# Transposes moved from TensorE to VectorE blocks and SBUF copies, with channels-first block ends in layer 0

## The chip, the cores and the metric

The kernel runs on one core of a Trainium2 chip. A core has four compute engines: TensorE (PE) for products, VectorE (DVE), ScalarE (ACT) and GpSimd (POOL). A fifth one, SyncE (SP), issues all copies of this kernel from one queue; 16 DMA engines carry them out. Everything is float32. The metric is device time in microseconds (us).

## The reference, cut to what matters

`x` is 4 images of 128 channels by 4096 positions. Layer 0 is an attention over all positions with a gate. Layer 1 is a second attention whose queries and keys are the same tensor, then a recurrence over all positions.

```python
# layer 0 (per image; n, m run over 4096 positions)
xn   = group_norm(x, 32 groups)
v, g = split(sigmoid(bn(Wvg @ xn)))             # 128 channels each
q, k = bn(Wq @ xn) * 64**-0.5, bn(Wk @ xn)      # 64 channels each
attn = softmax(einsum('bdn,bdm->bnm', q, k))
x    = x + bn(Wp @ (einsum('bcm,bnm->bcn', v, attn) * g))
# layer 1, on tokens t = transpose(x): (image, position, channel)
h  = layernorm(t);  q = h @ W
t  = t + softmax(q @ q.T) @ h
Wx = batch_norm(layernorm(t) @ Wf.T)            # over all images and positions
# y_i = sigmoid(Wx_i + y_(i-1) @ V.T), i over positions in order
x  = transpose(t + ys)
```

## The kernel before, in words

The work on each image is cut into 8 blocks of 512 query positions (`QB`; four tiles of 128, `NQ`). The images follow each other: `group_norm`, `project` (q, k, v, gate), `layer0`, `layer1`. After the last image comes the recurrence, called the scan here.

**Layer 0** (`attention`). For each block n there are 16 pair steps. In each, PE makes two score products `ps` (L186), ACT takes the exponential `e` (L189), VectorE adds it into `acc` (L198) for the denominators, and PE weighs the values into `o` (L326), two steps behind (`LAG`). Five buffers hold `e`. The end of a block is cut into closures that `finish` puts into the queue `pending`: `sums`, `residual`, `tokens`, `turn`, `queries`. The loop takes one out in every second pair step, in the middle of the next block, so that their work lies among the products. Every engine runs its own instructions in order; a waiting one holds up all behind it on that engine. The order on each engine is laid out when the program is built.

In `sums`, the 512 denominators are brought onto partitions by four products with one column of ones (`md`, L214). `residual` turns the four 128x128 tiles of x + bias on PE (`mx`, L351). `tokens` projects with positions first, four products (`mt`, L357), scales by the reciprocal denominators, stores the tokens into HBM (`t_d`) and normalises them (`h`). `turn` turns `h` back on PE (`mh`, L372), and `queries` makes the layer-1 queries `qt` from it (`mq`, L377). After the last block the queue is flushed with nothing beside it.

**Layer 1.** Scores are symmetric, so only the tiles a <= n of the 8x8 grid of blocks are computed (`ps`, L502; `e`, L508; `o`, L404). An off-diagonal tile is also used transposed: VectorE turns `e` in 32x32 blocks into `dd` (L513), 16 copies within SBUF put the blocks in place as `tt` (L532), and PE multiplies by it (`ot`, L417), while VectorE sums its rows into `slots` (L422). There are 28 such tiles per image. A finished block queues `tokens` (4 turns on PE, `mt`, L456), `result` (4 turns, `mr`, L467, and a copy to `t2_d` in HBM), `turn` (4 turns, `mh`, L475) and `inputs` (`mw`, L480, into `wxs`). These steps are taken from the same queue, also during the next image's `project`.

**The scan.** Positions are cut into 128 stretches of 32 that run side by side for all images; each starts from a state got by 12 warm-up steps on the end of the stretch before it. In each of the 44 steps and for each half of the images, PE adds `vt @ y` to a PSUM bank that VectorE has filled with the scaled inputs (L598), and ACT takes the sigmoid (L615).

Of the kernel before, what the change touches and what calls it, by code (L numbers as in the profile page):

```python
# [9 lines left out]
F32 = mybir.dt.float32  # L10
I32 = mybir.dt.int32
AF = mybir.ActivationFunctionType
ALU = mybir.AluOpType
# [21 lines left out]
L, W = 32, 12  # L35
# [13 lines left out]
def conv_attn_hybrid_kernel(  # L49
# [14 lines left out]
    t_d = dram.tile([B, NB, P, NQ, C], F32, name="t_d")  # L64
# [33 lines left out]
    ones = const.tile([P, 1], F32, name="ones")  # L98
# [9 lines left out]
    def inv_sqrt(dst, var, eps):  # L108
# [6 lines left out]
        tc, x, out, t_d, t2_d,  # L115
# [6 lines left out]
    with ExitStack() as st:  # L122
        ps = st.enter_context(tc.tile_pool(name="ps_f", bufs=1, space=PSUM))
        bad = const.tile([1, 1], I32, name="bad")
        n_ok = ps.tile([1, 1], F32, tag="f", name="n_ok")
        nc.tensor.matmul(n_ok, lhsT=par_ok[:, 0:1], rhs=ones, start=True, stop=True)
        nc.vector.tensor_scalar(bad, n_ok, P - 0.5, None, ALU.is_lt)
# [9 lines left out]
def fast(  # L137
    tc, x, out, t_d, t2_d, wt, col, par, bpc, bc, ident, gavg, ones, shift, inv_sqrt, par_ok
# [5 lines left out]
    wxs = keep.tile([P, L // 2, B, G, 2], F32, name="wxs")  # L144
    bn_st = keep.tile([P, B * NB, 6], F32, name="bn_st")
    den_all = keep.tile([P, 2 * B * NT], F32, name="den_all")

    with ExitStack() as st:
# [60 lines left out]
        def denominators(acc, at, rinv):  # L209

            nc.vector.tensor_tensor(acc[:, 0, :], acc[:, 0, :], acc[:, 1, :], ALU.add)
            m = ps_m.tile([P, NQ], F32, tag="m", name="md")
            for j in range(NQ):
                nc.tensor.matmul(  # L214
                    m[:, j : j + 1], lhsT=acc[:, 0, bass.ts(j, P)], rhs=ones,
                    start=True, stop=True,
                )
            den = den_all[:, at : at + NQ]
            nc.vector.tensor_copy(den, m)
            nc.vector.reciprocal(rinv, den)  # L220

        def layernorm(src, dst):
# [3 lines left out]
            for j in range(NQ):  # L226
                s6 = stat.tile([P, 6], F32, tag="s6", name="s6")
                nc.vector.bn_stats(s6, src[:, j, :])  # L228
                nc.vector.bn_aggr(mv[:, j, :], s6)  # L229
            inv_sqrt(rstd, mv[:, :, 1], EPS_LN)  # L230
            for j in range(NQ):
                nc.vector.tensor_scalar(  # L232
                    dst[:, j, :], src[:, j, :], mv[:, j, 0:1], rstd[:, j : j + 1],
                    ALU.subtract, ALU.mult,
                )
# [75 lines left out]
        def layer0(b, gate, q, k, v):  # L311
# [20 lines left out]
            def finish(n, o, acc):  # L332
# [5 lines left out]
                rinv = stat.tile([P, NQ], F32, tag="rinv", name="rinv")  # L338
                xb = work.tile([P, QB], F32, tag="xb", name="xb", bufs=2)
                t = work.tile([P, NQ, C], F32, tag="t", name="t", bufs=2)  # L340
                ht = work.tile([P, QB], F32, tag="th", name="ht")
                nc.sync.dma_start(xb, x[b, :, cs])
                nc.gpsimd.tensor_scalar(xb, xb, bpc, None, ALU.add)  # L343

                def sums():
                    denominators(acc, b * NT + n * NQ, rinv)

                def residual():
                    m = ps_m.tile([P, NQ, P], F32, tag="m", name="mx")
                    for j in range(NQ):  # L350
                        nc.tensor.transpose(m[:, j, :], xb[:, bass.ts(j, P)], ident)  # L351
                    nc.scalar.copy(t, m)

                def tokens():
                    m = ps_m.tile([P, NQ, P], F32, tag="m", name="mt")
                    for j in range(NQ):
                        nc.tensor.matmul(  # L357
                            m[:, j, :], lhsT=og[:, bass.ts(j, P)], rhs=wt["ps"],
                            start=True, stop=True,
                        )  # L360
                    for j in range(NQ):
                        nc.vector.scalar_tensor_tensor(
                            t[:, j, :], m[:, j, :], rinv[:, j : j + 1], t[:, j, :],
                            ALU.mult, ALU.add,
                        )
                    nc.sync.dma_start(t_d[b, n], t)
                    layernorm(t, h[:, ts, :])

                def turn():
                    m = ps_m.tile([P, QB], F32, tag="m", name="mh")  # L370
                    for j in range(NQ):
                        nc.tensor.transpose(m[:, bass.ts(j, P)], h[:, n * NQ + j, :], ident)  # L372
                    nc.scalar.copy(ht, m)

                def queries():
                    m = ps_m.tile([P, QB], F32, tag="m", name="mq")
                    nc.tensor.matmul(m, lhsT=wt["a"], rhs=ht, start=True, stop=True)  # L377
                    nc.scalar.copy(qt[:, cs], m)  # L378

                pending.extend([sums, residual, tokens, turn, queries])  # L380
# [4 lines left out]
        def layer1(b, h, qt):  # L385
# [55 lines left out]
            def finish(n):  # L441
                cs = bass.ts(n, QB)
                rinv = stat.tile([P, NQ], F32, tag="rinv", name="rinv")
                t = work.tile([P, NQ, C], F32, tag="t", name="t1", bufs=2)
                h2 = work.tile([P, NQ, C], F32, tag="h2", name="h2")
                th = work.tile([P, QB], F32, tag="th", name="th")
                nc.sync.dma_start(t, t_d[b, n])

                def tokens():
                    at = (B + b) * NT + n * NQ  # L450
# [3 lines left out]
                    m = ps_m.tile([P, NQ, P], F32, tag="m", name="mt")  # L454
                    for j in range(NQ):
                        nc.tensor.transpose(m[:, j, :], oacc[:, n, bass.ts(j, P)], ident)  # L456
                    for j in range(NQ):
                        nc.vector.scalar_tensor_tensor(  # L458
                            t[:, j, :], m[:, j, :], rinv[:, j : j + 1], t[:, j, :],
                            ALU.mult, ALU.add,  # L460
                        )
                    layernorm(t, h2)

                def result():
                    m = ps_m.tile([P, QB], F32, tag="m", name="mr")
                    for j in range(NQ):
                        nc.tensor.transpose(m[:, bass.ts(j, P)], t[:, j, :], ident)  # L467
                    t2 = work.tile([P, QB], F32, tag="xb", name="t2", bufs=2)
                    nc.scalar.copy(t2, m)
                    nc.sync.dma_start(t2_d[b, :, cs], t2)  # L470

                def turn():
                    m = ps_m.tile([P, QB], F32, tag="m", name="mh")
                    for j in range(NQ):
                        nc.tensor.transpose(m[:, bass.ts(j, P)], h2[:, j, :], ident)  # L475
                    nc.scalar.copy(th, m)

                def inputs():
                    m = ps_m.tile([P, QB], F32, tag="m", name="mw")
                    nc.tensor.matmul(m, lhsT=wt["f"], rhs=th, start=True, stop=True)  # L480
                    nc.vector.bn_stats(bn_st[:, b * NB + n, :], m)
                    nc.vector.tensor_copy(
                        wxs[:, :, b, bass.ts(n, GB), :],
                        m.rearrange("p (g i s) -> p i g s", i=L // 2, s=2),
                    )

                pending.extend([tokens, result, turn, inputs])
# [62 lines left out]
        ok = stat.tile([P, 2, 2 * B * NT], F32, tag="ok", name="ok", bufs=1)  # L550
        nc.vector.tensor_scalar(ok[:, 0, :], den_all, DEN_LO, None, ALU.is_ge)
        nc.vector.tensor_scalar(ok[:, 1, :], den_all, DEN_HI, None, ALU.is_le)
        nc.vector.tensor_reduce(par_ok[:, 1:2], ok.rearrange("p a b -> p (a b)"), AX.X, ALU.min)


    with ExitStack() as st:
        scan = st.enter_context(tc.tile_pool(name="scan", bufs=1))
        ps_r = st.enter_context(tc.tile_pool(name="ps_r", bufs=1, space=PSUM))
# [3 lines left out]
        y = scan.tile([P, L // 2, B, G, 2], F32, name="y")  # L562
        state = scan.tile([P, B, G + 1], F32, name="state")
        nc.gpsimd.memset(state[:, :, 0:1], 0.0)

        HB = B // 2
        banks = [[ps_r.tile([P, 512], F32, tag=f"r{s}{i}", name="ps_r") for i in range(3)] for s in range(2)]
        for s in range(2):  # L570
            for i in range(3):
                nc.tensor.matmul(
                    banks[s][i][:, : HB * G], lhsT=ident, rhs=wxs[:, 0, :HB, :, 0],
                    start=True, stop=True, skip_group_check=True,
                )
# [8 lines left out]
        nc.vector.tensor_sub(bias, col(BETA), bias)  # L584

        halves = [slice(s * HB, (s + 1) * HB) for s in range(2)]
        steps = list(range(L - W, L)) + list(range(L))

        def bank(k, s):
            return banks[s][k % 3][:, : HB * G].rearrange("p (b g) -> p b g", g=G)  # L590

        def at(tile_, i, bs):
            return tile_[:, i // 2, bs, :, i % 2]

        def preload(k):
            if k < len(steps):
                for s, bs in enumerate(halves):
                    nc.vector.tensor_scalar(bank(k, s), at(wxs, steps[k], bs), gain, None, ALU.mult)  # L598

        todo: deque = deque()  # L600
        preload(1)
        preload(2)
        for k, i in enumerate(steps):
            for s, bs in enumerate(halves):

                dst = state[:, bs, 1:] if k == W - 1 else at(y, i, bs)
                if k == 0:
                    nc.scalar.activation(dst, at(wxs, i, bs), AF.Sigmoid, bias=bias, scale=gain)
                    continue
                before = state[:, bs, :G] if k == W else at(y, i - 1, bs)  # L610
                nc.tensor.matmul(
                    bank(k, s), lhsT=wt["vt"], rhs=before, start=False, stop=True,
# [428 lines left out]
```

## Time and profile before

| what | us |
|---|---|
| median of 3 runs (3354.44 to 3355.76) | 3355.1 |
| the profiled execution | 3355.76 |
| its span, first to last instruction | 3353.9 |
| first layer-0 score, image 0 | 54.7 |
| first layer-1 score, image 0 | 438.8 |
| first layer-0 score, image 1 | 867.0 |
| first activation of the scan | 3268.6 |

How to read it: the page's first part gives the busy time of each engine as a share of the span. The chain is the work that ended last, followed back through what released each step. In the groups, "line engine op, out<-in, shapes, xcount" is followed by busy time, mean ns of one, and idle time just before them with what ended it; busy time counts overlap once, so it can be less than count times mean. SPq in a timeline is the SP engine's queue, and its time is the time to issue copies, not to move the data. "128*128 128x512" is a product with 128 rows of contraction and a 128x512 result. A float32 product appears as two records.

### The profile page before, as it was taken

The numbers are of one execution on the slowest core, as the hardware profiler recorded it, in microseconds if no ns is written. First come the engines' busy times: TensorE is split into PE (matmuls) and PEld (weight loads), VectorE is DVE, ScalarE is ACT, GpSimd is POOL, SyncE is SP. The second block draws the span as 40 slices with busy tenths as digits, with TensorE's granted clock in tenths as the row PEclk, the third lists the DMA queues.
The fourth block names the chain that finished last, engine by engine and source line by source line (L and its number), as shares of the span: only waits on it lengthen the run. The fifth ranks groups of instructions, "written<-read, shape, count | busy, mean of one in ns | idle before, by whom it ended". The sixth has DMA issues, their size and how long they took to land.

```text
span 3353.9 us, 32409 instructions
## 1 busy us (share of the span) xinstructions
PE 3148.9 (94%) x11210; PEld 1437.9 (43%) x11210; DVE 1708.3 (51%) x2793; ACT 1171.5 (35%) x2050; POOL 144.1 (4%) x183
## 2 busy tenths in 40 slices
PE   6999999997899999999699999999979999999976
PEld 3444444443444444444344444444434444444433
DVE  4545544555555544555645554455555555345556
ACT  3443432332434333233244343323233444332324
POOL 0000000000000000000000000000000000000000
PEclk9999999998999999999899999999989999999998
DMA  1000023332000003333200001333300000233334
GB/s 41 13 10 10 10 70 90 92 91 88 10 10 13 13 13 88 91 90 92 67 7 13 13 7 35 90 95 93 102 26 13 7 13 10 63 91 92 91 97 175
DMA packets 109084, 179.24 MB, mean 53 GB/s; under 512 B 31472, under 2 KB 31984, under 8 KB 107888
## 3 DMA queue, kind: packets, MB, share of 16 engines
q1 hardware_dynamic: 108912, 177.08, 19.4%
q8 instruction: 92, 1.51, 0.2%
q14 instruction: 80, 0.66, 0.1%
HBM read 34.35 MB, written 25.17 MB: 18 GB/s over the span
## 4 chain that ended last, share of the span: by engine, by line
PE 88%; DVE 6%; ACT 2%; POOL 1%; issue 1%; DMA 1%; SPq 0%; DVEq 0%; POOLq 0%; ACTq 0%
PE o L326 26%; PE ps L186 14%; PE ps L502 14%; PE o L404 14%; PE ot L417 11%; PE mq L377 1%; PE pvg L293 1%; PE mt L357 1%; POOL rstd L111 1%; PE md L214 1%; PE mw L480 1%; PE pvg L297 1%; DMA xg<-in_x_dram 1%; DVE t L458 1%; DVE s L228 1%
## 5 line engine op out<-in xcount | busy, mean ns | idle before, releaser
L326 PE MATMUL o<-e,v 64*128 64x512 f32 x4096 | 960.1, 590 | 0.0
L198 DVE TENSOR_TENSOR acc<-acc,e 128x1024 f32<-128x1024 f32 x448 | 548.7, 1225 | 525.3 <-ACT e L189 519.5
L189 ACT ACTIVATE e<-ps 128x1024 f32<-128x1024 f32 x512 | 521.0, 1024 | 684.5 <-PE ps L186 684.5
L508 ACT ACTIVATE e<-ps,shift 128x512 f32<-128x512 f32 x576 | 391.2, 683 | 940.1 <-PE ps L502 768.3
L326 PEld LDWEIGHTS o<-e,v 64*128 64x128 f32 x4096 | 397.3, 188 | 486.6 <-issue 479.0
L502 PE MATMUL ps<-qt 128*128 128x512 f32 x1152 | 547.3, 604 | 2.7 <-ACT qt L378 2.7
L186 PE MATMUL ps<-q,k 64*128 64x512 f32 x2048 | 539.5, 608 | 9.0 <-ACT e L189 4.8
L404 PE MATMUL o<-e,h 128*128 128x512 f32 x1152 | 527.7, 592 | 0.0
L417 PE MATMUL ot<-tt,h 128*128 128x512 f32 x896 | 402.8, 592 | 0.0
L513 DVE STREAM_TRANSPOSE dd<-e 128x512 f32<-128x512 f32 x448 | 285.7, 683 | 125.1 <-ACT e L508 82.4
L502 PEld LDWEIGHTS ps<-qt 128*128 128x128 f32 x1152 | 217.6, 194 | 269.9 <-issue 240.0
L404 PEld LDWEIGHTS o<-e,h 128*128 128x128 f32 x1152 | 217.1, 191 | 260.2 <-issue 260.2
L186 PEld LDWEIGHTS ps<-q,k 64*128 64x128 f32 x2048 | 185.6, 187 | 223.1 <-issue 123.2
L417 PEld LDWEIGHTS ot<-tt,h 128*128 128x128 f32 x896 | 170.2, 190 | 214.3 <-issue 212.4
L422 DVE TENSOR_REDUCE slots<-tt 128x4 f32<-128x2048 f32 x112 | 252.9, 2258 | 2.3 <-DMA tt<-dd 1.7
L429 DVE TENSOR_TENSOR oacc<-oacc,ot 128x512 f32<-128x512 f32 x84 | 57.4, 684 | 309.7 <-PE ot L417 309.7
L232 DVE TENSOR_SCALAR h<-t,mv,rstd 128x128 f32<-128x128 f32 x256 | 73.0, 346 | 94.5 <-POOL rstd L111 94.4
L508 ACT ACTIVATION_READ_ACCUMULATOR e<-ps,shift 128x1 f32 x576 | 113.0, 196 | 0.0
L343 POOL TENSOR_SCALAR xb<-xb,bpc 128x512 f32<-128x512 f32 x32 | 57.0, 1781 | 1112.4 <-DMA xb<-in_x_dram 1112.4
L110 POOL TENSOR_SCALAR rstd<-mv 128x4 f32<-128x4 f32 x64 | 14.6, 229 | 1949.0 <-DVE mv L229 1949.0
L427 DVE COPY oacc<-ot 128x512 f32<-128x512 f32 x28 | 19.4, 692 | 139.5 <-PE ot L417 139.5
L293 PE MATMUL pvg<-w_vs,xg 128*128 128x128 f32 x256 | 42.7, 318 | 31.9 <-ACT xg L304 23.8
(112 smaller groups left out, 1510.9 us busy)
## 6 DMA issues: line engine op xcount, KB each, us to landing
tt<-dd SPq DMA_DIRECT2D x1792, 64.0 KB, 2.0
t_d<-t SPq DMA_DIRECT2D x64, 256.0 KB, 2.0
xg<-in_x_dram SPq DMA_DIRECT2D x16, 512.0 KB, 5.6
xb<-in_x_dram SPq DMA_DIRECT2D x32, 256.0 KB, 2.7
t<-t_d SPq DMA_DIRECT2D x32, 256.0 KB, 2.7
t2s<-t_d SPq DMA_DIRECT2D x4, 2048.0 KB, 14.8
out_dram<-t2s SPq DMA_DIRECT2D x4, 2048.0 KB, 15.6
w<-in_wts_dram SPq DMA_DIRECT2D x1, 512.0 KB, 3.5
```

Source lines behind the costliest of these rows:

```text
L186: nc.tensor.matmul(ps[:, h, :], lhsT=lhsT, rhs=rhs, start=True, stop=True)
L189: nc.scalar.activation(e, ps, AF.Exp, scale=scale)
L198: nc.vector.tensor_tensor(acc, acc, e, ALU.add)
L232: nc.vector.tensor_scalar(dst[:, j, :], src[:, j, :], mv[:, j, 0:1], rstd[:, j : j + 1], ALU.subtract, ALU.mult,)
L293: nc.tensor.matmul(pv[:, 0, bass.ts(i, P)], lhsT=xg[:, bass.ts(4 * ch + i, P)], rhs=wt["vs"], start=True, stop=True,)
L326: nc.tensor.matmul(o[r], lhsT=v[rs, p + h * PAIRS, :], rhs=e[rs, h, :], start=(p == 0 and h == 0), stop=(p == PAIRS - 1 and h == 1),)
L404: nc.tensor.matmul(o, lhsT=h[:, NQ * a + 2 * i + half, :], rhs=e[:, half, :], start=(a == n and i == 0 and half == 0), stop=(a == 0 and i ...
L417: nc.tensor.matmul(ot, lhsT=h[:, NQ * n + j, :], rhs=t[:, :, j, :, :].rearrange("q p k j -> q k p j"), start=(j == 0), stop=(j == NQ - 1),)
L422: nc.vector.tensor_reduce(slots[:, bass.ts(n, NQ), a], t.rearrange("q p b k j -> q b p (k j)"), AX.XY, ALU.add,)
L502: nc.tensor.matmul(ps[:, half, :], lhsT=qt[:, bass.ts(at, P)], rhs=qt[:, bass.ts(n, QB)], start=True, stop=True,)
L508: nc.scalar.activation(e[:, half, :], ps[:, half, :], AF.Exp, bias=shift, accum_out=slots[:, at, n : n + 1],)
L513: nc.vector.transpose(d.rearrange("q f b k j -> q k b f j")[:, 2 * i + half], e[:, half, :].rearrange("q (b f j) -> q b f j", b=NQ, f=NQ),)
```

## The change

All transposes of tokens leave PE. A new function `move` turns a 128x512 tile on VectorE in 32x32 blocks into `d` (two buffers), and, where a destination is given, sends 16 copies of 32 partitions x 128 elements to put the blocks in place:

```diff
+        def move(blocks, dst):
+            d = work.tile([P, 4, NQ, 32], F32, tag="d", name="d", bufs=2)
+            nc.vector.transpose(d.rearrange("q a j i -> q j a i"), blocks)
+            if dst is not None:
+                for p in range(4):
+                    for a in range(4):
+                        nc.sync.dma_start(dst[bass.ts(a, 32), p], d[bass.ts(p, 32), a])
+            return d
```

Layer 0's block end stays channels first up to the residual. One product with a full matrix of ones puts the sums on all partitions, the reciprocal is taken over 128x512, and one product projects. Two moves follow, for `t` and for `ht`:

```diff
                 def sums():
-                    denominators(acc, b * NT + n * NQ, rinv)
-                def residual():
-                    (4 transposes of xb on PE, copy by ACT into t)
+                    nc.vector.tensor_tensor(acc[:, 0, :], acc[:, 0, :], acc[:, 1, :], ALU.add)
+                    m = ps_m.tile([P, QB], F32, tag="m", name="md")
+                    nc.tensor.matmul(m, lhsT=ones, rhs=acc[:, 0, :], start=True, stop=True)
+                    rinv = work.tile([P, QB], F32, tag="h2", name="rinv")
+                    nc.vector.reciprocal(rinv, m)
+                    nc.sync.dma_start(rinv_d[b * NB + n : b * NB + n + 1, :], rinv[0:1, :])
+                    nc.vector.tensor_tensor(og, og, rinv, ALU.mult)
+                def project_out():
+                    m = ps_m.tile([P, QB], F32, tag="m", name="mt")
+                    nc.tensor.matmul(m, lhsT=wt["ps"], rhs=og, start=True, stop=True)
+                    nc.vector.scalar_tensor_tensor(xb, m, bpc, xb, ALU.add, ALU.add)
+                    move(xb.rearrange("c (j f k) -> c j f k", j=NQ, f=4), t)
                 def tokens():
-                    (4 products mt on PE, 4 scalings on VectorE)
                     nc.sync.dma_start(t_d[b, n], t)
-                    layernorm(t, h[:, ts, :])
-                def turn():
-                    (4 transposes of h on PE, copy by ACT into ht)
+                    layernorm([t[:, :, j, :] for j in range(NQ)], [...])
+                    move(h[:, ts, :].rearrange("q j (p i) -> q j p i", p=4), ht)
-                pending.extend([sums, residual, tokens, turn, queries])
+                pending.extend([sums, project_out, tokens, queries])
```

Lines in brackets stand for the removed code. The addition of the bias to `xb` on POOL goes too, and `xb` has one buffer in place of two. In layer 1 a block end has three turns by VectorE: `oacc` into `ot` (name `otk`; 16 copies), `t` straight to HBM (16 copies with runs of 128 bytes), and `h2` into `th` (16 copies):

```diff
+                def weighted():
...
+                    move(oacc[:, n, :].rearrange("c (j f k) -> c j f k", j=NQ, f=4), ot)
                 def tokens():
...
+                    d = move(t.rearrange("q p j i -> q j p i"), None)
+                    to = t2_d[b, :, cs].rearrange("(p i) (j f k) -> i p j f k", p=4, f=4, j=NQ)
+                    for f in range(4):
+                        for p in range(4):
+                            nc.sync.dma_start(to[:, p, :, f, :], d[bass.ts(f, 32), p])
+                    layernorm([t[:, :, j, :] for j in range(NQ)], [...])
+                    move(h2.rearrange("q j (p i) -> q j p i", p=4), th)
-                pending.extend([tokens, result, turn, inputs])
+                pending.extend([weighted, tokens, inputs])
```

The denominators of layer 0 are checked from the rows stored in HBM (`rinv_d`), read back before the scan. The scan has 16 warm-up steps (`W`) in place of 12, a plain layout of `wxs` and `y`, and PE in place of VectorE adds the scaled inputs:

```diff
-L, W = 32, 12
+L, W = 32, 16
-                    nc.vector.tensor_scalar(bank(k, s), at(wxs, steps[k], bs), gain, None, ALU.mult)
+        nc.vector.tensor_scalar(dgain, ident, gain, None, ALU.mult)
+                ps = ps_r.tile([P, HB, G], F32, tag=f"r{s}", name="ps_r")
+                nc.tensor.matmul(ps, lhsT=dgain, rhs=wxs[:, i, bs, :], start=True, stop=first, ...)
+                if not first:
+                    nc.tensor.matmul(ps, lhsT=wt["vt"], rhs=befores(bs), start=False, stop=True, ...)
+                nc.scalar.activation(outs(bs), ps, AF.Sigmoid, bias=bias)
```

The additions of `y` to the tokens come four together at every fourth step, in place of one a step.

## The prediction

> **What bounds the kernel now.** I read the page first: busy shares, then the chain that ended last, then the costliest groups, then the DMA issues.
>
> ```profile
> PE 3148.9 (94%) x11210; PEld 1437.9 (43%) x11210; DVE 1708.3 (51%) x2793; ACT 1171.5 (35%) x2050; POOL 144.1 (4%) x183
> PE 88%; DVE 6%; ACT 2%; POOL 1%; issue 1%; DMA 1%; SPq 0%; DVEq 0%; POOLq 0%; ACTq 0%
> ```
>
> TensorE (PE) is the bound: 94% busy and 88% of the chain. Taking products off it pays only while nothing makes it wait. The groups of instructions, shapes kept apart, price what leaves it and what comes:
>
> ```profile
> L404 PE MATMUL o<-e,h 128*128 128x512 f32 x1152 | 527.7, 592 | 0.0
> L357 PE MATMUL mt<-w_ps,og 128*128 128x128 f32 x256 | 36.9, 287 | 3.5 <-DVE og L337 3.5
> L214 PE MATMUL md<-ones,acc 128*128 128x1 f32 x256 | 33.7, 253 | 0.0
> L351 PE MATMUL mx<-ident,xb 128*128 128x128 f32 x128 | 20.9, 285 | 1.4 <-DVE den_all L219 1.4
> L513 DVE STREAM_TRANSPOSE dd<-e 128x512 f32<-128x512 f32 x448 | 285.7, 683 | 125.1 <-ACT e L508 82.4
> ```
>
> A float32 product is two records, so a 512-wide product costs 527.7/576 = 0.92 us. A 32x32-block transpose of a 128x512 tile costs VectorE 0.68 us.
>
> The resource the change leans on is not in the busy shares at all: SP's queue, which issues every copy. The timeline of SP alone, in layer 1, and the tile view of `tt`:
>
> ```profile
> 600.07 10.01 SPq L532 DMA_DIRECT2D tt<-dd  x16
> ...
> L532 SPq DMA_DIRECT2D tt<-dd x1792: 507/589/1771, 452.7 to 3231.1; - x200
> ...
> DMA to landing us min/median/max: 1.9/2.0/4.0
> ```
>
> Sixteen SBUF-to-SBUF copies keep SP for 10.0 us (0.625 us each with the gap); each lands 2.0 us after its issue. One off-diagonal tile of layer 1 gives PE 12 products (11.0 us by 0.92; 10.3 at the 0.86 of a gapless stream), so SP is already nearly full there. Its issues are 28 x 10.0 = 280 us of each image's layer 1, which lasts 428 us from its first score (438.8) to the next image's first layer-0 score (867.0).
>
> The timeline of PE at a layer-0 block end shows the room for a moved step:
>
> ```profile
> 158.24 1.16 PE L357 MATMUL mt<-w_ps,og 128*128 128x128 f32 x8
> ...
> 170.61 1.13 PE L377 MATMUL mq<-ht,w 128*128 128x512 f32 x2
> ```
>
> From `mt` to `mq` PE has 11 us of other work, in which LayerNorm and one turn are hidden.
>
> **What the Trainium skill says.** (1) "VectorE: DVE Perf Modes", The three transpose paths: VectorE turns only 32x32 blocks, so the grid of blocks needs another step, here 16 copies. The trace agrees: `dd` is followed by exactly that. (2) "DMA: Bandwidth & Descriptors", Issuing engines are not separate DMA queues: issue time on the sequencer is "usually small relative to the DMA itself". The trace differs for these copies, 10.0 us of issue against 2.0 us to land; the measurement decides. (3) "VectorE: DVE Perf Modes", Walkthrough: reciprocal is an iterative divide with repeat count 8. No wide reciprocal is in the trace. (4) "TensorE: Matmul & The Clock Gate", Part 1: after about 3.4 us idle the array runs at half rate until it has been busy about as long. The trace agrees: after the layer boundary 12 score records took 8.21 us instead of 12 x 0.43 = 5.2.
>
> **The change part by part.** Sums are against the profiled execution (3355.8 us, span 3353.9), 0.7 us above the median.
>
> *Layer 0, PE work.* Gone per block: md, mx, mt and mh, (33.7 + 20.9 + 36.9 + 23.3)/32 = 3.6 us. New: two 512-wide products, 1.8. Net -1.8 us.
>
> *Layer 0, sums.* VectorE now does a 128x512 reciprocal and a product between `md` and `mt`. Bounds for the reciprocal: 0.7 us as any 128x512 operation (692 ns), 4.4 us by the skill's eight passes (estimate: 8 x 512 x 1.04 ns + 0.15). The 128x4 one took 178 ns against 163 for a 128x4 copy, some 4 ns more per element, so I take 2.5. In the compiled order VectorE does reciprocal, gate product, first `acc` (waits for e), then og*rinv: 5.2 us after `md`; PE has two score pairs and one weighing, 3.4 us. PE waits 1.8 us (0.8 to 3.7).
>
> *Layer 0, the two moves.* From the end of `mt`: xb 0.75, transpose 0.75 (at 1.5 us), 16 copies of 16 KB on SP 10.0, last landing 1.4 after that: `t` is there at 13.1. VectorE stands at bn_stats for it, in order, with the later `acc` additions queued behind; ACT would feel that only when five e buffers are full, ten pairs in, later than the stop below. LayerNorm is 3.8 us (160.5 to 164.3), one `acc` 1.2 and the second transpose 0.7: 18.9. Then 16 copies and landing: `ht` at 30.5. The compiled order puts five pairs (5 x 2.575 = 12.9 us) between `mt` and `mq`. PE therefore stands 17.6 us at `mq`, then restarts cold: +2 (estimate from the 3 us above). Cover: there is none; the pending queue was spaced for 11 us. Interior block: 17.6 + 1.8 + 2.0 - 1.8 = +19.6; 28 of them, **+549**.
>
> *Layer 0, last block of an image.* Nothing runs beside it. Before: 12.9 us from the last weighing (425.9) to the first score (438.8). After: md 0.9, reciprocal 2.5, two products 1.4, mt 1.1, xb and transpose 1.5, move 12, LayerNorm 3.8, transpose 0.8, move 12, cold mq 2.1, copy 1.3: 39.6. Four times +26.7, **+107**.
>
> *Layer 1.* PE loses 12 turns per block (72.5 us in all), worth nothing if SP is the bound. SP gains 48 copies per block (`otk`, t2 to HBM, `th`): 384 per image beside 448. 832 x 0.625 = 520 us, +5 for loads. To that: 14 us until the first tile is ready, as before (438.8 to 452.7); SP idle where it waits for VectorE: 1.3 us in each of five early blocks (`ot` landing, four 0.28 us operations and a transpose, 3.6 us, against 3.1 us of tile copies between), about 5 us in each of the last six tiles, where the reduction of the tile before stands ahead of the transposes (2.3 + 2.7), 3.6 in the last three blocks: 48; landing 2. Sum 589 against 428: +161 for three images. Project and the next group norm fall inside this, because their loads and their VectorE work stand between the last moves. The last image has no project beside it: 590 + 12.6 to the scan's first activation against 390 (2878.7 to 3268.6): +213. **+696.** What else hangs on the longer queue: the next tile's `tt`, so PE's `ot`, and VectorE's `mw` reads, behind which the next tile's transposes stand.
>
> *Scan.* Sixteen warm-up steps for 12, and PE does four 256-wide products a step in place of two, VectorE's preload gone. At the gapless 0.43 us that is 1.72 us a step, more than the 1.29 to 1.38 of now (ACT's activation plus product), so PE bounds it: 48 x 1.72 = 83 against 60. **+23** (15 to 35).
>
> *Costed at nothing.* Four 0.59 us ACT copies a block go (75 us in all; ACT is 35% busy and not on the path), and POOL's 1.8 us bias addition (57 us, POOL 4% busy). The row store of rinv is one more issue per block in layer 0, where SP has 33 issues (21 us) in a block of over 40. One `xb` buffer in place of two makes the x load wait for the transpose of the block before, half a block ahead of its use. Checks on the rows before the scan: 3 us if nothing covers them.
>
> Sum: 549 + 107 + 696 + 23 = 1375: 4731 us, 4730 on the median's scale.
>
> **The unknown size** is the issue time of the new copies: same form and partitions as `tt`, a quarter of the bytes; t2 has 128-byte runs into HBM. Lower bound 0.33, what a 128-partition store to HBM took (319 to 330 ns); upper 0.8, for the short runs (a guess inside what the trace has: the 2 MB stores at the end took 337 to 1187 ns to issue). At 0.36: waits at `mq` 9.1, layer 0 +384, layer 1 +299: 4060. At 0.8: layer 0 +180, layer 1 +270 on the forecast: 5180. I take 0.625, since `tt` is the only row with both ends in SBUF.
>
> **Rivals.** *A, cheap issues* (0.33 to 0.4): about 4060. For it: the HBM stores; against: 1792 copies that never took under 507 ns. *B, lockstep in layer 1:* SP, VectorE and PE wait for each other at every tile, 5 us of SP idle in all 28: 22 more tiles x 5 x 4 = +440, 5170. For it: orders were laid out for other durations; against: copies queued ahead keep SP fed. *C, faster:* the moves hide, and PE keeps its 128 us (56 + 72), less 23 in the scan: 3250. It decides from the issue time: two moves must fit 12.9 us, 32i + 2.8 + 7.3 < 12.9, so i < 0.09 us; the least issue anywhere is 0.32. *D, no change:* VectorE or SP work only fills gaps; it would need i near 0.1 too.
>
> **How the numbers follow.** Forecast (0.5 to 0.75 us per issue, SP-bound) 0.66, A 0.12, B or dearer issues 0.19, C 0.02, D 0.01. The range 4180 to 5330 leaves out half of A and the far end of B. A measurement of this kernel tells 0.2% from no change. Faster 0.02, same 0.01, slower 0.97.
>
> **What would show it.** Right: SP issue of `t`, `ht`, `otk`, `th` near 10 us per 16; PE idle before `mq` near 17 us, released by DMA; in layer 1, SP nearly without gaps and PE idle before `ot` and `mw`; PE's share down to about 65%; scan 1.7 us a step. Wrong: 16 new copies in under 6 us, `mq` without a wait, or layer 1 under 480 us. The reciprocal's own row settles its price.

## The result, and the profile after

The changed kernel takes 4603.9 us (median of 4 runs, 4600.3 to 4606.0) where the kernel before takes 3355.0 us beside it: a ratio of 1.372, 95% interval 1.370 to 1.375. The forecast was 4730 us, with a range from 4180 to 5330. The profiled execution has a span of 4601.1 us against 3353.9.

The first lines to read are those that carried the bound before: the busy shares and the chain that ended last, on the page of the changed kernel.

```profile
PE 3264.8 (71%) x10382; PEld 1420.8 (31%) x10382; DVE 1896.7 (41%) x2774; ACT 1096.1 (24%) x1930; POOL 87.1 (2%) x151
SPq 40%; PE 38%; DVE 11%; DMA 5%; issue 4%; ACT 1%; POOL 1%; DVEq 0%
SPq L220 22%; SPq L524 14%; PE o L327 13%; PE ps L189 6%; PE ps L494 4%; SPq L462 4%; PE o L399 4%; PE ot L412 3%; DVE rinv L350 2%; PE mq L370 1%; DVE d L216 1%; DMA ht<-d 1%; DMA t<-d 1%; PE mt L356 1%; PE ps_r L580 1%
```

PE's share of the span fell from 94% to 71%, and of the chain from 88% to 38%. In its place stands SPq, the queue that issues copies, with 40%; before it had none. L220 is the copy inside `move` (22%), L524 the `tt` copies that were there before (14%), L462 the stores of t2 (4%). PE's busy time even rose, by 116 us, although it has fewer products: after a long pause it runs slowly for a while. The granted clock is 0.50 in the 5.2 us after one such pause, and over the whole span it is 0.85 on average against 0.972 before.

The groups of the changed kernel, shapes kept apart, say where PE stands idle. The last numbers of a row are the idle time just before its instructions and what ended it.

```profile
L399 PE MATMUL o<-e,h 128*128 128x512 f32 x1152 | 525.0, 592 | 0.0
L350 DVE RECIPROCAL rinv<-md 128x512 f32<-128x512 f32 x32 | 107.1, 3347 | 0.0
L370 PE MATMUL mq<-ht,w 128*128 128x512 f32 x64 | 65.5, 1126 | 576.2 <-DMA ht<-d 576.2
L471 PE MATMUL mw<-th,w 128*128 128x512 f32 x64 | 56.1, 974 | 284.5 <-DMA th<-d 282.9 <-issue 0.8 <-DVE gdev L259 0.8
L356 PE MATMUL mt<-og,w_ps 128*128 128x512 f32 x64 | 49.3, 862 | 83.0 <-DVE og L352 83.0
```

A plain layer-1 product costs what it did (592 ns a record). But PE waits 576 us before `mq`, which is 18 us for each of 32 blocks, always for the copies into `ht`; 83 us before `mt`, for the product that follows the reciprocal; and 284 us before `mw`. One reciprocal takes 3.35 us.

A timeline of one interior block of layer 0 (start us, duration, engine, line, operation, count; in brackets the idle time before it) shows the serial path:

```profile
167.23 3.35 DVE L350 RECIPROCAL rinv<-md 128x512 f32<-128x512 f32 x1
...
172.91 1.86 PE L356 MATMUL mt<-og,w_ps 128*128 128x512 f32 x2 [2.27 <-DVE og L352]
...
176.34 10.01 SPq L220 DMA_DIRECT2D t<-d  x16
...
193.72 10.01 SPq L220 DMA_DIRECT2D ht<-d  x16
205.09 2.04 PE L370 MATMUL mq<-ht,w 128*128 128x512 f32 x2 [16.33 <-DMA ht<-d]
```

From `mt` to `mq` it is 32.2 us, and 20 of them are two trains of 16 issues on SP. PE has five pairs of work for that stretch and then stands still for 16.3 us: the score products that stand behind `mq` in PE's order do not need it, yet begin only at 207.06 us, after it. Before, the same stretch had a turn on PE and a LayerNorm in it, and PE had work for all of it.

SP's own timeline in layer 1 has few gaps; the longest here is the 5.6 us before the stores of t2:

```profile
709.03 10.08 SPq L220 DMA_DIRECT2D otk<-d  x16
719.22 3.06 SPq L524 DMA_DIRECT2D tt<-dd  x5
727.90 8.22 SPq L462 DMA_DIRECT2D t_d<-d  x16
736.22 10.01 SPq L220 DMA_DIRECT2D th<-d  x16
746.27 58.63 SPq L524 DMA_DIRECT2D tt<-dd  x91
```

(The trace names t2's tile in HBM `t_d` too.) In the whole layer-1 stage of the first image, 550 us, SP waits 42 us. The longest of these waits (who waits for what: us in total, times, longest):

```profile
SPq L524 <- DVE dd L505: 19.1, 2, 17.7
SPq L462 <- DVE s L229: 17.3, 7, 7.7
SPq L462 <- DVE d L216: 4.2, 1, 4.2
```

Everything that a finished block adds, 28 us of issues, stands in the same queue as the `tt` copies that PE needs next.

By stage, each from first score to first score, the last to the scan's first activation:

| stage | before, us | after, us | in all | forecast |
|---|---|---|---|---|
| layer 0, four images | 384.1 | 555.7 to 559.1 | +693 | +656 |
| layer 1, three images | 428.3 | 550.1 to 551.8 | +367 | +483 |
| layer 1, last image | 392.7 | 556.8 | +164 | +213 |
| scan to the end | 85.3 | 108.8 | +23.5 | +23 |

The rows add up to the 1247 us between the two spans.

### The profile page after: what moved, and what is told of

Same layout as the page of the kernel before. It is cut to its first block, busy times and chain, and to the rows that moved or that the text cites. A ratio compares the mean times of both kernels' runs of the same rounds, so it can differ in the third digit from the quotient of the medians.

```text
span 4601.1 us, 33510 instructions
## 1 busy us (share of the span) xinstructions
PE 3264.8 (71%) x10382; PEld 1420.8 (31%) x10382; DVE 1896.7 (41%) x2774; ACT 1096.1 (24%) x1930; POOL 87.1 (2%) x151
## 3 DMA queue, kind: packets, MB, share of 16 engines
q1 hardware_dynamic: 276544, 210.92, 17.6%
## 4 chain that ended last, share of the span: by engine, by line
SPq 40%; PE 38%; DVE 11%; DMA 5%; issue 4%; ACT 1%; POOL 1%; DVEq 0%
SPq L220 22%; SPq L524 14%; PE o L327 13%; PE ps L189 6%; PE ps L494 4%; SPq L462 4%; PE o L399 4%; PE ot L412 3%; DVE rinv L350 2%; PE mq L370 1%; DVE d L216 1%; DMA ht<-d 1%; DMA t<-d 1%; PE mt L356 1%; PE ps_r L580 1%
## 5 line engine op out<-in xcount | busy, mean ns | idle before, releaser
L327 PE MATMUL o<-e,v 64*128 64x512 f32 x4096 | 982.6, 602 | 0.0
L189 PE MATMUL ps<-q,k 64*128 64x512 f32 x2048 | 571.4, 642 | 9.0 <-ACT e L192 4.8
L412 PE MATMUL ot<-tt,h 128*128 128x512 f32 x896 | 456.9, 658 | 154.9 <-DMA tt<-dd 149.6
L370 PE MATMUL mq<-ht,w 128*128 128x512 f32 x64 | 65.5, 1126 | 576.2 <-DMA ht<-d 576.2
L412 PEld LDWEIGHTS ot<-tt,h 128*128 128x128 f32 x896 | 185.5, 212 | 426.7 <-issue 422.0
L471 PE MATMUL mw<-th,w 128*128 128x512 f32 x64 | 56.1, 974 | 284.5 <-DMA th<-d 282.9
L370 PEld LDWEIGHTS mq<-ht,w 128*128 128x128 f32 x64 | 16.0, 311 | 604.7 <-issue 604.7
L373 ACT COPY qt<-mq 128x512 f32<-128x512 f32 x32 | 18.7, 585 | 690.4 <-PE mq L370 690.4
L229 DVE BATCH_NORM_STATS2 s<-t 128x6 f32<-128x128 f32 x256 | 63.9, 271 | 223.9 <-DMA t<-d 223.9
L474 DVE BATCH_NORM_STATS2 bn_st<-mw 128x6 f32<-128x512 f32 x32 | 22.3, 698 | 298.0 <-PE mw L471 298.0
```

The costliest lines, as they stand in the source:

```text
L189: nc.tensor.matmul(ps[:, h, :], lhsT=lhsT, rhs=rhs, start=True, stop=True)
L327: nc.tensor.matmul(o[r], lhsT=v[rs, p + h * PAIRS, :], rhs=e[rs, h, :], start=(p == 0 and h == 0), stop=(p == PAIRS - 1 and h == 1),)
L412: nc.tensor.matmul(ot, lhsT=h[:, NQ * n + j, :], rhs=t[:, :, j, :, :].rearrange("q p k j -> q k p j"), start=(j == 0), stop=(j == NQ - 1),)
```

## The experiments

The theory was that SP's time to issue a copy is what costs: in layer 0 as latency on a path that PE has too little work to cover, in layer 1 as SP's whole capacity. The rivals were that the copies' bytes or landings cost, or VectorE's longer work (the reciprocal, additions held in order). Ratios are to the kernel before on the same chip.

### Each part alone

Layer 0's block ends alone in the kernel before (`e2_l0_end`), layer 1's alone (`e3_l1_only`), the scan alone (`e4_scan_only`). Each is the corresponding function of the changed kernel put into the kernel before; in the first, the tile `t` keeps before's layout, so that the copies into it have 128-byte runs; in the second, layer 0 of before writes its tokens in the layout that the new layer 1 reads, and `xb` has one buffer.

> The kernel before with layer 0's block ends alone in the new way (the tile t stands in the order of before, so that the 16 copies into it have 128-byte runs). Theory (the parts add up, and each layer-0 block pays its own chain of copies): the four layer-0 stages were 173.3 us longer each in the changed kernel, so 3355 + 693 = 4048 us, with layer-1 stages of some 392 us as before. Rival (part of the excess of layer 0 comes from what the new layer 1 leaves behind: its copies still in SP's queue, its tiles still held): at least 30 us less than that, below 4018 us.

> The kernel before with the new block ends of layer 1 alone (oacc, t and h2 turned by VectorE, 48 copies a block). By the stage times, layer 1 grew by 122 us for each of three images and 164 for the last, 531 in all: about 3885 us if the parts add, with SP's queue without gaps over some 536 us an image and PE waiting before ot and mw for copies.

> The kernel before with the new scan alone: 16 warm-up steps, PE adding the scaled inputs. By the stage times +23.5 us: 3378, ratio 1.007. PE has four 256-wide products a step, 1.73 us a step. If VectorE's additions, 1.16 us each now against 0.68, held the steps, the steps that have them would be longer than the others.

Measured: 4063.3 us (ratio 1.211, 1.209 to 1.213), 3892.4 (1.160, 1.158 to 1.163) and 3381.8 (1.008, 1.007 to 1.010). Against 3355 that is 709, 538 and 27 us: 1274 together, where the whole change cost 1249. The parts add up to within 2%. Layer 0's stage is 4 us longer per image in the first of these than in the changed kernel; its cause was not followed up.

### Room in layer 0's queue of steps

```diff
-                pending.extend([sums, project_out, tokens, queries])
+                pending.extend([sums, project_out, idle, idle, tokens, idle, idle, queries])
```

> The changed kernel with four empty entries put into the pending queue of layer 0, so that PE has twelve pair steps (30.9 us) between mt and mq in place of five (12.9). Nothing else differs, and the copies are the same. Theory (two serial moves of 10 us of SP issue each are late only because the queue gives them too little room): PE's idle time before mq falls from 17 us to under 2 in the interior blocks, the cold restarts go too, and an interior block falls from 67.4 us to about 47; 28 x 20.4 = 571 less, about 4035 us. Layer 1, the last blocks and the scan stay. Rival (VectorE, which stands in order at bn_stats for t with the acc additions behind it, then stops ACT and PE through the five e buffers): PE gets new idle time before the scores, about 8 us a block, and the time stays above 4250.

Measured: 4060.4 us (ratio 1.210, 1.208 to 1.212), 543 us less than the changed kernel where 571 were expected, all of it in layer 0 (the four stages fell by 134 to 140 us each). The groups:

```profile
L373 PE MATMUL mq<-ht,w 128*128 128x512 f32 x64 | 39.5, 701 | 118.7 <-DMA ht<-d 118.2 <-issue 0.2
```

The wait before `mq` fell from 576 to 119 us, which is 29.0 to 29.5 us in each of the four last blocks, where nothing can cover it; in the interior blocks it is gone, and `mq` runs warm (701 ns a record instead of 1126). No copy was made cheaper: twelve pairs stand between `mt` and `mq` instead of five, and hide the same 20 us of issues. Latency without cover, not load, is what layer 0 lost.

### Half of each move on POOL's queue

```diff
-                        nc.sync.dma_start(dst[bass.ts(a, 32), p], d[bass.ts(p, 32), a])
+                        q = nc.sync if a % 2 == 0 else nc.gpsimd
+                        q.dma_start(dst[bass.ts(a, 32), p], d[bass.ts(p, 32), a])
```

> The changed kernel with half of the 16 copies of every move (a odd) issued by POOL instead of SP. Theory (what costs is the issue time of one queue, 16 x 0.589 us = 10.0 us a move): if an issue costs POOL what it costs SP, each move is over 5 us sooner, the wait before mq falls from 17.4 to about 7.4 us (-320 us over 32 blocks) and SP sheds 128 issues of 0.589 us per layer-1 stage (-302 us over four): about 3985 us. If an issue costs POOL 1.2 us, layer 0 gains nothing and layer 1 keeps its gain: about 4300 us. Rival (the copies are held by their landing, the DMA engines or the bytes, whoever issues): 4604 within 20 us.

Measured: 4134.9 us (ratio 1.233, 1.231 to 1.235), 469 us less. The rival is out: the same copies with the same bytes are faster when two queues issue them. The tile view of `ht` (duration min/median/max in ns) prices both queues:

```profile
L221 SPq DMA_DIRECT2D ht<-d x256: 512/590/601, 121.7 to 3535.8; - x128
L221 POOL DMA_DIRECT2D ht<-d x256: 496/498/581, 122.0 to 3535.2; - x128
```

The gain was 150 us short of the expectation, in two places. In layer 0 (-233, not -320) the path from `mt` to `mq` did shrink, from 31.7 to 22.4 us on average over the 28 interior blocks. But PE's order now has four pairs in that stretch where it had five; the pair of 2.57 us that was moved out of the cover is worth 72 us over these blocks, and the wait is 9.4 us on average instead of 7.4. In layer 1 (-238, not -302), the last image gained the expected 76 us, the other three 54 each; SP waits 55 us in the first of these, 13 more than in the changed kernel.

### One store of t2 instead of sixteen

```diff
-                    to = t2_d[b, :, cs].rearrange("(p i) (j f k) -> i p j f k", p=4, f=4, j=NQ)
-                    for f in range(4):
-                        for p in range(4):
-                            nc.sync.dma_start(to[:, p, :, f, :], d[bass.ts(f, 32), p])
+                    nc.sync.dma_start(t2_d[b, :, cs], d.rearrange("c p j i -> c (p j i)"))
```

> The changed kernel with one store of t2 per layer-1 block in place of 16: the same 256 KB to the same rows of t2_d, but in the order in which VectorE's blocks stand, so the reordering of these elements is left out. Theory (layer 1 is bounded by SP's issue time): 15 issues of 0.466 us less in each of 32 blocks, -224 us: about 4380 us. Rival (layer 1 is bounded by the bytes or the landings, or by the chain of VectorE's work): the bytes are the same, so 4604 within 25 us.

Measured: 4468.6 us (ratio 1.332, 1.330 to 1.335), 135 us less with the same bytes: 33 to 38 us per layer-1 stage where 56 were expected. The issues are part of the bound, but not all of what they took came free. SP's waits in the first layer-1 stage (who it waits for: us in total, times, longest) show why:

```profile
SPq L220 <- DVE d L216: 28.0, 8, 8.5
SPq L521 <- DVE dd L502: 19.4, 2, 17.6
```

The first row is new. SP reaches the copies into `th` before VectorE has finished the LayerNorm and turned `h2`; it stands 3.5 us in each of eight blocks, with the next `tt` copies behind it. In the changed kernel the train of t2 stores had covered that LayerNorm. All of SP's waits in this stage rose from 42 to 66 us, a little more than the 20 us that were missed.

### Five issues for sixteen, through HBM

```diff
-                for p in range(4):
-                    for a in range(4):
-                        nc.sync.dma_start(dst[bass.ts(a, 32), p], d[bass.ts(p, 32), a])
+                nc.sync.dma_start(s, d)            # s: one of 8 scratch tiles in HBM
+                sv = s.rearrange("(p r) a j i -> a r p (j i)", p=4)
+                for a in range(4):
+                    nc.sync.dma_start(dst[bass.ts(a, 32)].rearrange("r p j i -> r p (j i)"), sv[a])
```

> The changed kernel with every move going through a scratch tile in HBM: 1 store of the 256 KB and 4 loads (64 KB each, 512-byte runs) in place of 16 copies within SBUF; twice the bytes, two landings in a row, and 5 issues instead of 16. Theory (the number of issues on SP is what costs): 0.45 + 2.0 (landing) + 4 x 0.59 + 2.0 (landing) = 6.8 us in place of 10.0 + 2.0, so -5.2 us per move: -333 us over the 64 moves of layer 0, and in layer 1, where SP also has to wait for the store to land, 11 x 0.59 - 2.0 = 4.5 us less for each of 64 moves, -288 us: about 3985 us (3900 to 4250 as the landings are 1 to 4 us). Rival (bytes and landings cost, not issues): twice the bytes and one more landing make it slower than 4604 us.

Measured: 3950.9 us (ratio 1.178, 1.176 to 1.180), 653 us less, although each move now carries its bytes twice and lands twice. Layer 0 gave 343 of it (333 expected), layer 1 311 (288). SP's timeline in a layer-0 block:

```profile
281.77 0.34 SPq L222 DMA_DIRECT2D stage<-d  x1
282.15 0.43 SPq L349 DMA_DIRECT2D xb<-in_x_dram  x1
283.88 1.75 SPq L225 DMA_DIRECT2D t<-stage  x4
```

From the first issue to the last of a move it is 3.9 us where it was 10.0: the store costs 0.34 us to issue, the first load starts 1.8 us after that, and the four loads take 1.75. Here the issues are fewer and each is also cheaper than the 0.59 us of a copy within SBUF. That layer 0 came so near its expectation is in part luck: the path from `mt` to `mq` shrank by 12.9 us where 10.4 were expected, but here too PE's order has only four pairs in it, 2.57 us less cover. With `e5_pool_queue`, where the copies are the same, this settles the theory: what costs is the time in which SP issues them, not their bytes.

### The reciprocal

```diff
-                    nc.vector.reciprocal(rinv, m)
+                    nc.vector.tensor_copy(rinv, m)
```

> The changed kernel with the reciprocal over 128x512 (3.35 us on VectorE) replaced by a copy, so the division in layer 0 is left out. Theory (the reciprocal lies on the chain from the sums to mq, and its length is what TensorE waits for before mt): the chain is about 2.6 us shorter in each of 32 blocks (3.35 less 0.7 for the copy), and mt, no longer after a pause, runs warm: -75 to -95 us, about 4519 us. Rival (mt waits for the additions into acc that stand ahead on VectorE, or what is won before mt is lost again before mq): 4604 within 15 us.

Measured: 4520.6 us (ratio 1.347, 1.345 to 1.349), 83 us less, within 2 us of the expectation. The groups:

```profile
L370 PE MATMUL mq<-ht,w 128*128 128x512 f32 x64 | 65.4, 1126 | 598.0 <-DMA ht<-d 598.0
L356 PE MATMUL mt<-og,w_ps 128*128 128x512 f32 x64 | 36.0, 644 | 9.1 <-DVE og L352 9.1
```

The wait before `mt` falls from 83.0 to 9.1 us, and PE no longer restarts after it (644 ns a record instead of 862); 22 us come back as a longer wait before `mq` (598.0 instead of 576.2). So of the 1249 us some 80 are the reciprocal on the path from the sums to `mq`.

### A version from these

What was learnt says how layer 0's new order could pay: moves with few issues, and cover for every wait. `e9_staged_room` puts layer 0's block ends into the kernel before, with moves through HBM and room:

```diff
+                pending.extend([sums, idle, project_out, idle, tokens, idle, idle, queries])
```

> The kernel before with layer 0's block ends in the new way, the moves through a scratch tile in HBM (1 store and 4 loads), and four idle entries in the list of pending steps, one of them between sums and project_out, so that two more pairs of TensorE work lie before mt, and six more before mq. Layer 1 and the recurrence are those of before (t is read from t_d in 4 loads). Theory (with cover for the waits, what is left of the change in layer 0 is 1.8 us less TensorE work in each interior block and a longer end of the last block, 33.5 in place of 18.6 us): per image 7 x (-1.8) + 14.9 = +2.3 us, 3355 + 9 = 3364 us (3355 to 3385). Rival (the 3.35 us reciprocal and the layer norm hold VectorE's additions into acc, and so the e buffers and the exponentials, or mt waits all the same): +2 to +3 us in each of 28 interior blocks, 3420 us or more.

`e10_last_on_pe` adds to it, in `project_out` and likewise in `tokens`:

```diff
-                    move(xb.rearrange("c (j f k) -> c j f k", j=NQ, f=4), t)
+                    if n == NB - 1:
+                        m = ps_m.tile([P, NQ, P], F32, tag="m", name="mx")
+                        for j in range(NQ):
+                            nc.tensor.transpose(m[:, j, :], xb[:, bass.ts(j, P)], ident)
+                        nc.scalar.copy(t.rearrange("q p j i -> q j p i"), m.rearrange("q j (p i) -> q j p i", p=4))
+                    else:
+                        move(xb.rearrange("c (j f k) -> c j f k", j=NQ, f=4), t)
```

> The kernel e9_staged_room with the last block of each image turned by TensorE (4 transposes and a copy, twice) instead of by moves, since nothing covers the moves there. Theory (additivity; the end of the last block falls from 33.5 to some 24 us, which is before's 18.6 and the reciprocal and its product ahead of it): about 9.5 us less than e9_staged_room per image, -38 us: some 3326 us, under the 3355 us of the kernel before. Rival (the end of the last block is held by the reciprocal, the layer norm and POOL rather than by the moves): within 10 us of e9_staged_room.

> The same kernel as e10_last_on_pe, once more: one of its six executions took 7384 us where the others took 3341 to 3342. Theory (that one was a single event): 3341 us again in every execution. Rival (the kernel itself sometimes takes its second, general path, whose length is the 4042 us that came on top): again one or more of six executions at some 7384 us.

Measured: `e9_staged_room` 3379.6 us (ratio 1.007, 1.006 to 1.009), 15 us above its expectation. An interior block gained 1.5 us instead of 1.8, and each layer-1 stage is some 2 us longer than before. `e10_last_on_pe` 3341.3 us (ratio 0.9958, 0.9945 to 0.9971), and again as `e11_again` 3340.0 (0.9953, 0.9940 to 0.9967): 38 us under `e9_staged_room`, just the difference that was expected, and 0.4 to 0.5% faster than the kernel before, a small gain whose two intervals leave out 1. One of the eleven executions of this kernel took 7384 us. The program holds a second, general path behind a test of its denominators and of the scan, and it may have run, but no trace of that execution exists and no run shows the length of that path. It was not a lower clock: its granted clock is on record as 1.0, against 0.97 in the others. The cause stays open, and the version would have to be run more often before it could be relied on.

In the groups of `e10_last_on_pe`, PE's waits are gone except in the last blocks (19.6 us before `mt` is four times 4.9), with the 3.35 us reciprocal still in place:

```profile
L361 PE MATMUL mt<-og,w_ps 128*128 128x512 f32 x64 | 39.8, 707 | 19.6 <-DVE og L357 19.6
L396 PE MATMUL mq<-ht,w 128*128 128x512 f32 x64 | 39.8, 706 | 2.7 <-ACT ht L384 2.7
```

`e12_order_only` asks which half of the change this gain comes from: the same kernel, but with all of layer 0's transposes on PE, in two steps of their own, so that only the channels-first order is left.

```diff
-                pending.extend([sums, idle, project_out, idle, tokens, idle, idle, queries])
+                pending.extend([sums, idle, project_out, spread, tokens, idle, turn, queries])
```

> The kernel e10_last_on_pe with the transposes of all of layer 0's blocks on TensorE (8 of 128x128 per block, in steps of their own), so that of the change only the channels-first order, the sums on all partitions and the one projection product are left. Theory (what e10_last_on_pe wins over the kernel before is the TensorE time of the transposes, 0.63 + 0.66 us a block): +1.3 us in each of 28 interior blocks, 3341 + 36 = 3377 us, slower than before by the longer end of the last blocks (24.1 in place of 18.6 us). Rival (the gain lies in the order and the single product, not in who transposes): 3341 to 3350 us, still under the 3355 us of before.

Measured: 3381.6 us (ratio 1.0076, 1.0063 to 1.009), 40 us over `e10_last_on_pe`, in line with the theory. Its groups show what PE has back:

```profile
L383 PE MATMUL mh<-ident,h 128*128 128x128 f32 x128 | 23.0, 306 | 15.4 <-DVE h L238 15.4
L367 PE MATMUL mx<-ident,xb 128*128 128x128 f32 x128 | 22.8, 305 | 3.4 <-DVE xb L362 3.4
```

That is 45.8 us of transposes against 9.1 us in `e10_last_on_pe`. So the aim of the change, transposes off PE, is worth some 40 us in layer 0 if their copies are few and covered. The order by itself costs, by its longer last block: 24.2 us from the last score to layer 1's first, against 18.6; an interior block takes 46.5 us, as in the kernel before.

## Why the prediction was right, point by point

- **The bound moves from PE to SP's queue.** Right: SPq 40% of the chain, PE 71% busy (about 65% was named). PE's share came out higher for the reason that its work after pauses runs slowly and counts as busy, and because the span is shorter than forecast.
- **16 copies in SBUF take SP 10.0 us.** Right, at 16 KB as at 64 KB: 10.01 us per train for both. The forecast set this against the statement in the Trainium skill, "DMA: Bandwidth & Descriptors", Issuing engines are not separate DMA queues, that issue time is usually small beside the transfer, but it compared sixteen issues with one landing. For a single copy the issue is 0.59 us and the landing 2.0, so the trace does not contradict the page there. What counts is the sum: the issues of a train follow each other on SP, and the last copy of the train at 176.34 us has landed 1.3 us after them. Sharing the issues with a second queue (`e5_pool_queue`) and cutting their count (`e8_staged`) both showed it.
- **Layer 0, 17.6 us before `mq`.** Right: 16.4 us on average over the 28 interior blocks. An interior block came out 20.9 us longer (67.4 against 46.5 on average, from one block's first score to the next one's) instead of 19.6.
- **The reciprocal, 2.5 us.** Mis-sized: 3.35 us, inside the bounds of 0.7 and 4.4. The upper bound came from the eight passes in the Trainium skill, "VectorE: DVE Perf Modes", Walkthrough; measured is 3347/512 = 6.5 ns per element. `mt` waits 2.27 us where 1.8 was taken, and the slow restart after that wait was not in the sum at all. In the block shown `mt` takes 1.86 us, about 0.75 more than a warm pair of records, and the first scores after it 2.04 instead of 1.13; in 9 of the 28 interior blocks it ran warm (1.12 us), in the other 19 it took up to 2.02. On average the restart costs 1.1 us. `e7_no_reciprocal` priced reciprocal, wait and restart together at 83 us.
- **The restart after `mq`, 2.0 us.** Low: at 137.2 us `mq` takes 2.05 us for 1.12, the first scores 2.08 for 1.13, the first weighing 2.56 for 1.88. They overlap a little: together it is 2.5 us, in that block and on average. That PE restarts slowly after a stop of 16 us agrees with the Trainium skill, "TensorE: Matmul & The Clock Gate", Part 1. The stop before `mt` is only 2.27 us, less than the 3.4 us that the page names, and yet slow products followed it in most blocks (granted clock 0.54 from 172.9 to 176.5 us). Together, on average: 16.4 and 2.3 us of waits, 2.5 and 1.1 of restarts, less 1.8 of work, 20.5 us a block (measured 20.9) where the forecast had 19.6. The wait before `mt` and the two restarts were 2.1 us too small in it and the wait before `mq` 1.2 too large; over 28 blocks the difference is most of the +37 us by which layer 0 was under-forecast.
- **The last blocks, +26.7 us each.** Right in the sum: 45.5 to 45.9 us from the last score to layer 1's first, against 18.6, is +26.9 to +27.3. Some of that is luck. In the first image the reciprocal and the cold `mt` took 1.8 us more than their terms, and the first move and the copy after `mq` 1.4 us less. (The terms listed add up to 39.4 us, not 39.6.)
- **Layer 1, +696 us.** Right in mechanism, 165 us too much. Two terms were mis-sized. The price 0.625 us was used for all new issues, but the stores of t2 cost less (tile views of `ht` and of t2's tile in HBM):

```profile
L220 SPq DMA_DIRECT2D ht<-d x512: 507/589/702, 125.8 to 3930.9; - x171
```

```profile
L462 SPq DMA_DIRECT2D t_d<-d x512: 303/430/2003, 727.9 to 4471.9; - x171
```

  A train of 16 of them takes 7.45 us or somewhat more: up to 2.5 us less for each of 8 blocks, some 20 us per stage. And SP waits only 42 us in a stage where the forecast had 62 (14 at the start and 48 for VectorE). Together they are about the 39 us per stage by which three of the stages came out shorter. The last image's stage is 556.8 us instead of 603. SP waits 39 us there, so the same two terms explain most of the 46 us; the rest was not taken apart. Before the change that stage was 392.7 us, not the 390 of the forecast, which began it at 2878.7 us where the first score is at 2875.9.
- **Scan, +23 us.** Right: +23.5, and `e4_scan_only` gave +27 by itself (+23.2 from the scan's first activation to the end). The price of 1.72 us a step holds: the four products of a step follow each other at 0.43 us.
- **Rivals.** Cheap issues (4060 us) and no change or faster needed issues under 0.4 and 0.1 us; only t2's stores came near the first. Lockstep in layer 1 (5170 us) would show SP idle at every tile; it waits 42 us in 550. The forecast's 4060 us for cheap issues should be some 4050: at 0.36 us an issue its terms for layer 1 give +289, not +299.

## What to carry to other kernels

In this kernel a copy's price is not its bytes but the time that it takes in the queue that issues it: sixteen copies within SBUF held SP for 10 us at 16 KB each and at 64 KB each. Before moving work from a busy engine to copies, count the issues, add them on the queue that already carries copies on the path, and ask how many microseconds of other work lie between the step and its reader; layer 0's part of the change cost 693 us without cover and gained 0.4% with five issues for sixteen, cover in the step queue, and the uncovered last block left on PE. When a train of issues goes away, look at what it had been covering: the next wait on the same queue can take part of the gain, as in `e6_t2_one`, where SP waited 24 us more in a stage. Look at the order of the other engines too: with the faster moves of `e5_pool_queue` and `e8_staged` one pair of products left the cover.

## What was not expected of the hardware

- POOL issues a copy within SBUF in 0.50 us, no slower than SP with 0.59.
- A 256 KB store of 128 partitions to HBM costs SP 0.34 us to issue, a 64 KB load of 32 partitions 0.42, a 16 KB store with 128-byte runs 0.43, a copy from SBUF to SBUF 0.59 whether 16 or 64 KB.
- In the scan, the additions into `t2s` with 32-element steps in the innermost dimension take VectorE 1.16 us, where the pairs of adjacent elements in the kernel before took 0.68. In the groups of the changed kernel:

```profile
L606 DVE TENSOR_TENSOR t2s<-t2s,y 128x512 f32<-128x512 f32 x32 | 34.9, 1161 | 53.6 <-ACT y L589 53.6
```

- A float32 reciprocal over 128x512 from PSUM takes 3.35 us, 4.9 times a copy of the same shape (0.68 us in `e7_no_reciprocal`).
